# A graph layer's gather: one tile of source rows by TensorE products in two of three blocks

## The chip, the cores and the metric

The kernel runs on one core of a Trainium2 chip. The metric is the device time of one execution in microseconds (us). Three runs of the kernel before give 3887.06 us as their median (3886.89 to 3891.37).

## The reference

There are 6250 nodes with 128 features and 200,000 edges sorted by their target `dst`. Layer 0 is a graph attention layer with 8 heads of 16, layer 1 a message passing layer; each has a layer norm and a ReLU ahead of it and is added to `x`.

```python
h = relu(layernorm(x))
z = (h @ W).reshape(N, 8, 16);  el, er = sums of z * attn_l, z * attn_r over each head
e = leaky_relu(el[src] + er[dst], 0.2)
a = exp(e - segment_max(e, dst)[dst])
x = x + segment_sum(z[src] * a, dst) / max(segment_sum(a, dst), 1e-9) + bias
h = relu(layernorm(x))
sv = h @ W_up                                    # scalars and vectors of each node
w  = silu(silu(edge_feats @ A1 + b1) @ A2 + b2) @ A3
x = x + (segment_sum(products of sv[src], edge_attrs and w, dst) / 10) @ W_out
```

## The kernel before

The edges are cut into 1563 tiles of 128, and 16 tiles make a block: 98 blocks, the last one with 11 tiles. Nodes lie in 50 tiles of 128 rows (the first is shifted by 32 rows). A first stage writes the table `t0` (6368 rows of 136 numbers: z and el of each node) to DRAM. Layer 0 then runs over the blocks, writes node rows `sv` to the tables `t1` and `t1z`, and layer 1 runs over the blocks with `t1`.

What both layers spend on getting `z[src]` matters here. For each edge tile POOL issues one indirect DMA (`gather`, L833), which fetches the 128 rows that the tile's source indices name. In every third block from 3 to 95 (`by_row`) the last tile is fetched in another way: SP loads 32 row addresses at a time into registers (L1074) and issues 128 DMAs of one row each (L1078), into the buffer `r`; ACT copies them into the block's `z` (`filled`). `rows_until` spreads these DMAs over SP's program: at each half iteration it emits rows until the count for three blocks ahead is reached. `r` has three buffers, `z` five (and `z_first`).

In layer 0 the order of PE, DVE, ACT and SP is the order of the program. Iteration g of the loop works at several blocks at once, each in a later stage: 

- It starts POOL's gathers for block g+3 (`take_rows`).
- SP emits rows, the stores of a finished node tile (`node_out`, L1298, of the tile from the iteration before), the load of a tile of x (`node_rows`, L1239) and more rows.
- Block g gets its logits (`logits`: DVE adds el and er, PE transposes) and the running maxima within a segment (`maxima`, two scans on DVE).
- Block g+1 (`n1`) gets er of each edge's target. `turned` transposes the one-hot tiles `s` on PE (L1151, into `p_d`) and ACT casts them to bf16 as `d` (L1153); `er_of` multiplies `d` with er, kept as three bf16 terms (L1162); `er_sum` adds the terms.
- Block g+2 (`n2`) gets its one-hot tiles s on DVE (`ends_of`, L1097), which say which of the block's 128 targets each edge has.
- Block g-1 (`b4`) gets the maxima of its neighbours, the weights a (`weights`), z times a on DVE (`weighted`, L1229) and the sums over the targets on PE (`sums`, L1234, into `p_u`).
- Block g-2 is closed (`ended`); every second block ends a node tile, which is normalised and multiplied with W_up (`node_x` to `node_s`).

All rows of x stay in SBUF (`x_all`) from layer 0 to layer 1.

Of the kernel before, what the change touches and what calls it, by code (L numbers as in the profile page):

```python
# [741 lines left out]
def tile_even_edges(  # L742
# [88 lines left out]
    def gather(to, table, tiles, width, first=0):  # L831
        for k, t in enumerate(tiles, first):
            nc.gpsimd.indirect_dma_start(  # L833
                out=to[:, k, :width], out_offset=None, in_=table,
                in_offset=bass.IndirectOffsetOnAxis(ap=src_col[:, t : t + 1], axis=0))
        return to
# [128 lines left out]
def even_edges(tc, v):  # L965
# [7 lines left out]
    with ExitStack() as ctx:  # L973
        const = ctx.enter_context(tc.tile_pool(name="fconst", bufs=1))
        z_pool = ctx.enter_context(tc.tile_pool(name="fz", bufs=5))
        s_pool = ctx.enter_context(tc.tile_pool(name="fs", bufs=16))
# [18 lines left out]
        x_all = const.tile([P, NX, P], F32, name="fx_all")  # L995
# [8 lines left out]
        a3p = const.tile([P, 2, P], F32, name="fa3p")  # L1004
        nc.sync.dma_start(a3p, v["a3p"])
# [4 lines left out]
        wout = const.tile([P, 2, P], F32, name="fwout")  # L1010
        nc.sync.dma_start(wout, v["wout"])
        dloc = const.tile([P, NB * KB], F32, name="fdloc")
        identb = l0c.tile([P, P], BF, name="fidentb")
        nc.vector.tensor_copy(identb, ident)
# [8 lines left out]
        with tc.tile_pool(name="fbuild", bufs=1) as build:  # L1023
            d_c = build.tile([P, TU], I32, name="fd_c")
            nc.sync.dma_start(d_c, dstc)
            d_i = build.tile([P, TG, P], I32, name="fd_i")
            nc.sync.dma_start(d_i, tiles_of(dstt, P))
            q_i = build.tile([P, TG, P], I32, name="fq_i")
            nc.sync.dma_start(q_i, tiles_of(dstt, P - 1))
            nxt_i = build.tile([P, TG], I32, name="fnxt")  # L1030
            nc.sync.dma_start(nxt_i, tiles_of(dstt, 2 * P)[:, :, 0])
            off = build.tile([P, TU], F32, name="foffs")
            nc.sync.dma_start(off, nums[:, :TU])
            nc.vector.tensor_sub(dloc[:, :TU], d_c, off)


            eq = build.tile([P, TG, MC], F32, name="feq")
            nc.vector.tensor_tensor(eq[:, :, :P], d_i, q_i, OP.is_equal)
            nc.vector.memset(eq[:, :, 0:1], 0.0)
            nc.vector.memset(eq[:, :, P : P + 1], 0.0)  # L1040
            nc.vector.tensor_tensor(eq[:, :, P + 1 : 2 * P + 1], d_i,
                                    nxt_i.unsqueeze(2).to_broadcast([P, TG, P]), OP.is_equal)
            nc.vector.tensor_tensor(eq[:, :, 2 * P + 1 :], d_i,
                                    q_i[:, :, 0:1].to_broadcast([P, TG, P]), OP.is_equal)
            for g in range(TG):
                nc.scalar.activation(masks[:, g, :], eq[:, g, :], AF.Copy, bias=-BIG, scale=BIG)

            zeros = build.tile([P, NL, P], F32, name="fzeros")
            nc.vector.memset(zeros, 0.0)
            nc.sync.dma_start(t1z[LATE * P - W0 :].rearrange("(j p) f -> p j f", p=P), zeros)  # L1050
# [5 lines left out]
        with tc.tile_pool(name="fat_ps", bufs=1, space=PSUM) as at_ps:  # L1056
            col = l0c.tile([P, P], F32, name="fcol")
            n = NB - 1
            nc.vector.tensor_copy(col[:, :n], v["src_col"][:, KB - 1 : n * KB : KB])
            p_c = at_ps.tile([P, P], F32, name="p_c")  # L1060
            nc.tensor.transpose(p_c[:n], col[:, :n], ident)
            for i, w in enumerate((ZW, P)):
                nc.vector.tensor_scalar(at[i][:n], p_c[:n], float(4 * w), None, op0=OP.mult)
# [53 lines left out]

        in_order = {mybir.EngineType.PE, mybir.EngineType.DVE, mybir.EngineType.Activation,
                    mybir.EngineType.SP}
        with tc.manual_schedule(engines=in_order), \  # L1120
                tc.tile_pool(name="l0", bufs=2) as l0, \
                tc.tile_pool(name="l0n", bufs=2) as l0n, \
                tc.tile_pool(name="l0_ps", bufs=1, space=PSUM) as l0_ps:
# [3 lines left out]
            p_n = l0_ps.tile([P, 512], F32, name="p_n")  # L1127
            er_p, iota_p = p_n[:, P : 2 * P].rearrange("p (t h) -> p t h", h=H), p_n[:, 3 * P :]
            nc.scalar.copy(iota_p, iota)

# [14 lines left out]

            def turned(c, q):
                if 4 * q < c["kt"]:
                    m = min(4, c["kt"] - 4 * q)
                    p_d = l0_ps.tile([P, 4, P], F32, name="p_d", bufs=2)
                    for k in range(m):  # L1150
                        nc.tensor.transpose(p_d[:, k, :], c["s"][q][:, k, :], ident)  # L1151
                    d = c["d", q] = l0.tile([P, 4, P], BF, name="d", bufs=4)
                    nc.scalar.copy(d[:, :m], p_d[:, :m])  # L1153
# [17 lines left out]
            def logits(c, bank="pe"):  # L1171
                kt = c["kt"]
                kr = kt * H
                e_s = l0.tile([P, KB, H], F32, name="e_s")
                pe = c["pe"] = p_n if bank == "p_n" else l0_ps.tile([P, 512], F32, name=bank, bufs=2)
                nc.vector.tensor_add(e_s[:, :kt], c["z"][:, :kt, F:], c["er"][:, :kt])  # L1176
                nc.vector.scalar_tensor_tensor(e_s[:, :kt], e_s[:, :kt], 0.2, e_s[:, :kt],  # L1177
                                               op0=OP.mult, op1=OP.max)
                nc.tensor.transpose(pe[:kr, :P], e_s[:, :kt].rearrange("p t h -> p (t h)"), ident)  # L1179
# [57 lines left out]

            def node_rows(i, n):
                nc.sync.dma_start(x_all[:, i : i + n, :],  # L1239
                                  xp[i * P : (i + n) * P].rearrange("(j p) f -> p j f", p=P))  # L1240

            def with_bias(i, n):
                x_i = x_all[:, i : i + n, :]
                nc.vector.tensor_add(x_i, x_i, bias_b[:, None, :].to_broadcast([P, n, F]))

            def node_x(u):
                i, n, agg = u["i"], u["n"], u["agg"]
                x_i = x_all[:, i : i + n, :]
# [14 lines left out]
            def node_h(u):  # L1263
                i, n = u["i"], u["n"]
                rs, mr = normal(l0n, u["mv"], u["rs"], n, f"n{n}")
                xn = u["xn"] = l0n.tile([P, 2, P], F32, name="xn")
                nc.scalar.activation(xn[:, 0, :], x_all[:, i, :], AF.Identity, bias=mr[:, 0, :],
                                     scale=rs[:, 0, :])
                if n == 2:
                    nc.vector.tensor_scalar(xn[:, 1, :], x_all[:, i + 1, :], u["mv"][:, 1, 0:1],  # L1270
                                            rs[:, 1, :], op0=OP.subtract, op1=OP.mult)

            def node_t(u):
                n = u["n"]
                u["p_n"] = p_n.rearrange("p (j f) -> p j f", f=P)
                for j in range(n):
                    nc.tensor.transpose(u["p_n"][:, j, :], u["xn"][:, j, :], ident)
                h_t = u["h_t"] = l0n.tile([P, 2, P], F32, name="h_t")
                nc.scalar.activation(h_t[:, :n], u["p_n"][:, :n], AF.Relu)
# [11 lines left out]
            def node_out(u):  # L1291
                i, n, sv = u["i"], u["n"], u["sv"]
                first = i * P - W0
                for table in (t1, t1z) if i < LATE else (t1,):
                    if i == 0:
                        nc.sync.dma_start(table[: P - W0, :], sv[W0:, 0, :])
                    else:
                        nc.sync.dma_start(  # L1298
                            table[first : first + n * P].rearrange("(j p) f -> p j f", p=P), sv)

# [12 lines left out]
            def take_rows(g):  # L1313
                if 0 < g < NG:
                    c = cs[g]
                    t = c["b"] * KB + c["o"]
                    c["z"] = gathered(t0, range(t, t + c["kt"] - (c["b"] in by_row)), ZW)
# [28 lines left out]
            for g in range(1, 3):  # L1346
                take_rows(g)
            masks_of(cs[0])
# [12 lines left out]
            for i in range(2):  # L1361
                node_rows(i, 1)
            for g in range(NG - 3):
# [3 lines left out]
                for n in late:  # L1367
                    node_out(n)
                if g % 2 == 0 and g // 2 + 2 < NX - 2:
# [6 lines left out]
                logits(c)  # L1376
                ends_of(n2, 0)
# [3 lines left out]
                maxima(c)  # L1381
                ends_of(n2, 1)
# [5 lines left out]
                er_of(n1, 0)  # L1388
                if b4:
                    weights(b4)  # L1390
                for n in nodes:
# [3 lines left out]
                if b4:  # L1395
                    bank_of(b4)
                    weighted(b4, 0)
                turned(n1, 3)
                er_of(n1, 2)
                if b4:  # L1400
                    weighted(b4, 8)
                for n in nodes:
# [4 lines left out]
                if b4:  # L1407
                    sums(b4, 0)
                for n in nodes:
# [7 lines left out]
                if b4:  # L1417
                    sums(b4, 8)
                if g == NG - 4:
# [68 lines left out]
        with tc.manual_schedule(engines=in_order), \  # L1488
                tc.tile_pool(name="l1", bufs=3) as l1, \
                tc.tile_pool(name="l1n", bufs=2) as l1n, \  # L1490
                tc.tile_pool(name="l1_ps", bufs=2, space=PSUM) as l1_ps:

# [79 lines left out]

            def node1(i, agg):
                x_i = x_all[:, i, :]
# [10 lines left out]
            def node_out1(i):  # L1585
                x_i = x_all[:, i, :]
                if i == 0:
                    nc.sync.dma_start(out[: P - W0, :], x_all[W0:, 0, :])
# [54 lines left out]
            rows, rows_until.n, late = rows_by_row(1, t1, P), 0, []  # L1643
# [13 lines left out]
            for i, u in enumerate(us):  # L1657
                b, k0, m = u["b"], u["k0"], u["m"]
                if k0 == 0:
                    take_rows(b + 2)  # L1660
                    filled(1, b, blk[b]["z"], P)
                    edge_rows(b + 2)
                if k0 == 4:
# [43 lines left out]
            x_i = x_all[:, NX - 2 :, :]  # L1707
# [140 lines left out]
```

## Time and profile before

| | us |
|---|---|
| median of three runs | 3887.06 |
| the profiled execution | 3888.67 |
| its span, first to last instruction | 3886.9 |
| POOL busy / PE busy / DVE busy / ACT busy | 2913.0 / 2848.8 / 2224.5 / 1396.8 |
| layer 0's first logits / last block's gathers begin | 91.7 / 1945 |
| layer 1's first gather from `t1` | 1989.4 |
| mean granted clock of TensorE | 0.803 |

In the profile, PE is TensorE's matmuls, PEld its weight loads, DVE VectorE, ACT ScalarE, POOL GpSimd and SP SyncE; "SPq" marks a DMA that SP issues. Busy time leaves out the issuing of DMAs by SP. A line of a group reads: line of the kernel, engine, operation, output<-input, count, then busy us and mean ns of one, then the idle time of the engine just before and what ended it.

### The profile page before, as it was taken

Reading aid. Unit: us, or ns where it says so; the run is one execution under the profiler, and the core shown is the slowest. Engines: PE = TensorE matmul, PEld = TensorE weight load, DVE = VectorE, ACT = ScalarE, POOL = GpSimd, SP = SyncE. Lnnn points to the kernel's source line nnn. Section 1 sums busy time; section 2 is a strip of 40 time slices with the busy share of each in tenths; the row PEclk is TensorE's granted clock in tenths of the full one; section 3 lists DMA queues with packets and bytes.
Section 4 is the critical chain, followed back from the end, with each engine's and each line's share of the span. In section 5 each row is a group of like instructions: output and inputs, shape, how many; then the busy total and the mean of one; then the engine's idle time right before and its main releaser. Section 6 shows DMA issues by size and latency. Waiting matters only on the chain. (4 is left out here: it accounts for less than half of the span.)

```text
span 3886.9 us, 62701 instructions
## 1 busy us (share of the span) xinstructions
PE 2848.8 (73%) x14785; PEld 2401.2 (62%) x14785; DVE 2224.5 (57%) x5408; ACT 1396.8 (36%) x3612; POOL 2913.0 (75%) x3096
## 2 busy tenths in 40 slices
PE   3766666666666766666678888888877777778777
PEld 3656656656556656666666666666666556656665
DVE  5544444444444444444457777677766666666666
ACT  3323232323322323232324444444444444444443
POOL 6777777777777777777777777777777777777776
PEclk6666666666666566666689999999999999999999
DMA  6222222222222222222222222222222222222221
GB/s 181 59 64 64 62 64 64 64 62 64 62 64 62 64 61 64 62 64 62 61 61 61 61 62 62 62 62 62 62 62 62 62 62 61 63 60 63 61 61 50
DMA packets 195262, 252.65 MB, mean 65 GB/s; under 512 B 78656, under 2 KB 145088, under 8 KB 194880
## 3 DMA queue, kind: packets, MB, share of 16 engines
q0 software_dynamic: 98048, 207.27, 22.6%
q1 hardware_dynamic: 96544, 41.19, 4.1%
q8 instruction: 120, 1.97, 0.2%
q14 instruction: 262, 2.15, 0.2%
q10 hardware_dynamic: 288, 0.07, 0.0%
HBM read 234.73 MB, written 13.25 MB: 64 GB/s over the span
## 5 line engine op out<-in xcount | busy, mean ns | idle before, releaser
L833 POOL DMA_INDIRECT g<-ft,fsrc x3024 | 2856.7, 945 | 922.4 <-issue 858.3
L1570 PE MATMUL p_u<-mj,s 128*128 128x256 f32 x3126 | 789.9, 397 | 217.9 <-DVE mj L1562 216.5
L1570 PEld LDWEIGHTS p_u<-mj,s 128*128 128x128 f32 x3126 | 588.9, 196 | 385.7 <-DVE mj L1562 310.9
L1234 PE MATMUL p_u<-g,s 128*128 128x136 f32 x3062 | 597.8, 376 | 0.4 <-DVE g L1229 0.4
L1234 PEld LDWEIGHTS p_u<-g,s 128*128 128x128 f32 x3062 | 572.1, 279 | 0.5 <-DVE g L1229 0.4
L1537 ACT ACTIVATE p_w<-p_w,yb 128x64 f32<-128x64 f32 x1563 | 450.3, 288 | 121.5 <-PE p_w L1533 80.4
L1553 DVE TENSOR_TENSOR vy<-g,p_i 128x384 f32<-128x384 f32 x387 | 212.9, 550 | 366.6 <-DMA g<-ft,fsrc 258.0
L1533 PE MATMUL p_w<-fa3p,h 128*128 128x256 f32 x1564 | 412.0, 387 | 0.0
L1151 PE MATMUL p_d<-fident,s 128*128 128x128 f32 x1563 | 384.7, 411 | 0.0
L1533 PEld LDWEIGHTS p_w<-fa3p,h 128*128 128x128 f32 x1564 | 289.4, 195 | 118.1 <-issue 52.5
L1176 DVE TENSOR_TENSOR e_s<-g,p_n 128x128 f32<-128x128 f32 x96 | 27.5, 286 | 578.6 <-DMA g<-ft,fsrc 566.2
L1518 ACT ACTIVATE h<-p_h,fb 128x512 f32<-128x512 f32 x196 | 134.6, 687 | 573.2 <-PE p_h L1516 571.8
L1151 PEld LDWEIGHTS p_d<-fident,s 128*128 128x128 f32 x1563 | 312.4, 225 | 37.6 <-issue 26.3
L1144 ACT COPY mk<-p_m 128x385 f32<-128x385 f32 (+1 forms) x99 | 47.6, 481 | 781.3 <-PE p_m L1141 781.2
L1229 DVE TENSOR_TENSOR g<-g,pe 128x1024 f32<-128x1024 f32 x193 | 225.5, 1209 | 129.2 <-ACT g L1220 126.4
L1153 ACT CAST d<-p_d 128x512 bf16<-128x512 f32 x391 | 228.8, 586 | 192.0 <-PE p_d L1151 141.6
L1179 PE MATMUL pe<-fident,e_s 128*128 128x128 f32 x98 | 39.1, 399 | 326.2 <-DVE e_s L1177 326.2
L1097 DVE TENSOR_TENSOR s<-p_n,fdloc 128x512 f32<-128x512 f32 x391 | 266.1, 682 | 6.7 <-ACT sv L1289 3.4
L1097 DVE TENSOR_TENSOR s<-p_i,fdloc 128x512 f32<-128x512 f32 x391 | 266.1, 681 | 3.8 <-ACT p_i L1512 3.8
L1516 PE MATMUL p_h<-ft,fa1p 128*128 128x128 f32 x1568 | 217.2, 283 | 63.3 <-DMA ft<-in_e_f_dram 63.1
L1516 PEld LDWEIGHTS p_h<-ft,fa1p 128*128 128x128 f32 x1568 | 210.6, 198 | 83.9 <-issue 65.3
L1523 ACT ACTIVATE h<-p_h,fb 128x512 f32<-128x512 f32 x196 | 134.7, 687 | 307.1 <-PE p_h L1520 307.1
(202 smaller groups left out, 3344.3 us busy)
## 6 DMA issues: line engine op xcount, KB each, us to landing
r<-ft SPq DMA_DIRECT2D x3968, 0.5 KB
r<-ft SPq DMA_DIRECT2D x3968, 0.5 KB
g<-ft,fsrc POOLq DMA_INDIRECT x3024
ft<-in_e_f_dram SPq DMA_DIRECT2D x98, 64.0 KB
yb<-in_e_y_dram SPq DMA_DIRECT2D x98, 32.0 KB
fx_all<-in_e_xp_dram SPq DMA_DIRECT2D x48, 64.0 KB
out_dram<-fx_all SPq DMA_DIRECT2D x47, 64.0 KB
ft<-sv SPq DMA_DIRECT2D x46, 64.0 KB
```

Of the source, the lines that this page charges most:

```text
L833: nc.gpsimd.indirect_dma_start(out=to[:, k, :width], out_offset=None, in_=table, in_offset=bass.IndirectOffsetOnAxis(ap=src_col[:, t : t + ...
L1097: nc.vector.tensor_tensor(s[:, :m], iota[:, None, :].to_broadcast([P, m, P]), dloc[:, t : t + m].unsqueeze(2).to_broadcast([P, m, P]), OP. ...
L1151: nc.tensor.transpose(p_d[:, k, :], c["s"][q][:, k, :], ident)
L1153: nc.scalar.copy(d[:, :m], p_d[:, :m])
L1229: nc.vector.tensor_mul(zh, zh, p_a[:, k0 : k0 + m].unsqueeze(3).to_broadcast([P, m, H, D]))
L1234: nc.tensor.matmul(c["p_u"][:, :ZW], c["s"][k // 4][:, k % 4, :], c["z"][:, k, :], start=c["o"] + k == 0, stop=c["o"] + k == KT[c["b"]] - 1)
L1516: nc.tensor.matmul(p_h[:, q, :], a1p[:, q0 + q, :], c["ft"], start=True, stop=True)
L1523: nc.scalar.activation(h2, p_h, AF.Silu, bias=b2)
L1533: nc.tensor.matmul(w[:, k : k + n].rearrange("p k a u -> p (k a u)"), c["h2"][q // 4][:, q % 4, :], a3p[:, :n].rearrange("p k f -> p (k f) ...
L1537: nc.scalar.activation(w[:, k, ::2, :], w[:, k, ::2, :], AF.Copy, scale=c["yb"][:, k0 + k, 0:1])
L1553: nc.vector.tensor_mul(vy, v_n, y_p)
L1570: nc.tensor.matmul(blk[b]["p_u"][:, :MW], u["s"][:, k, :], u["mj"][:, k, :], start=k0 + k == 0, stop=k0 + k == KT[b] - 1)
```

## The change

In layer 0, blocks 28 to 92 that are not in `by_row` are `dense`: 44 blocks. Their tile 14 is no longer gathered. Its rows are computed by products of one-hot tiles with the table itself, which lies in SBUF as `t0s`, each number split into three bf16 terms.

- `node_tiles(g + 1)` loads two tiles of 128 table rows per iteration from DRAM, one iteration ahead; `split(g)` makes the three terms of them at the iteration's end (two copies on ACT, two subtractions on DVE). This goes on for the first 25 pairs.
- For a dense block, `spread` (PE) writes the tile's source indices across all partitions, folded into a third of the table; `ends_to` (DVE, twice) makes 17 one-hot tiles; `rows_of` (PE) runs 17 x 3 matmuls, each with up to three table tiles (408 columns) beside each other, into the PSUM bank `p_x`; `taken` (DVE) picks of the three thirds the right one and writes the tile's `z`. A block's first 27 matmuls run two iterations before its logits, the other 24 and `taken` one before.
- To free two PSUM banks, `turned` changes in all blocks: a table `ends` of local target numbers is written to DRAM once at the start (`d_b`); `ends_row(b)` loads the block's 16 x 128 numbers to every partition by a DMA on SP (4 KB to each of 128 partitions), two buffers; DVE compares them with each partition's own number and writes `d` in bf16. The transposes on PE and the casts on ACT are gone.
- To free SBUF, `x_all` is gone: tiles of x come in buffers, are stored to DRAM (`x1`) behind the node's stores and are loaded again in layer 1 (`node_rows1`). `a3p` and `wout` are loaded at the start of layer 1.
- `er_p` and the iota move to the bank `p_i`; `p_n` is allocated for each node.

```diff
+        dense = {b for b in range(NX // 2 + 2, NB - 4) if b not in by_row}
+            def ends_row(b):
+                if b < NB:
+                    to = ends_row.tiles[b] = l0.tile([P, KB, P], BF, name="er_d", bufs=2)
+                    g, j = divmod(b, P // KB)
+                    nc.sync.dma_start(to, ends[g : g + 1, j * KB : (j + 1) * KB, :].to_broadcast([P, KB, P]))
             def turned(c, q):
                 if 4 * q < c["kt"]:
                     m = min(4, c["kt"] - 4 * q)
-                    p_d = l0_ps.tile([P, 4, P], F32, name="p_d", bufs=2)
-                    for k in range(m):
-                        nc.tensor.transpose(p_d[:, k, :], c["s"][q][:, k, :], ident)
-                    d = c["d", q] = l0.tile([P, 4, P], BF, name="d", bufs=4)
-                    nc.scalar.copy(d[:, :m], p_d[:, :m])
+                    d = c["d", q] = l0.tile([P, 4, P], BF, name="d")
+                    k0 = c["o"] + 4 * q
+                    nc.vector.tensor_tensor(d[:, :m], ends_row.tiles[c["b"]][:, k0 : k0 + m],
+                                            node_p.unsqueeze(2).to_broadcast([P, m, P]), OP.is_equal)
+            def spread(c):
+                b = c["b"]
+                nc.tensor.matmul(at_p, key[:, b : b + 1].to_broadcast([P, P]), ident,
+                                 start=True, stop=True)
+            def ends_to(c, h):
+                n = half if h == 0 else NR - half
+                oh = c["oh", h] = ohs[:, h * half : (h + 1) * half, :]
+                nc.vector.tensor_tensor(
+                    oh[:, :n], at_p.unsqueeze(1).to_broadcast([P, n, P]),
+                    place[:, h * half : h * half + n].unsqueeze(2).to_broadcast([P, n, P]), OP.is_equal)
+            def rows_of(c, k0, n):
+                if k0 == 0:
+                    p_x = l0_ps.tile([P, 512], F32, name="p_x")
+                    c["p_x"] = p_x[:, : 3 * ZW].rearrange("p (r f) -> p r f", f=ZW)
+                for k in range(k0, min(k0 + n, NR)):
+                    i = order[k]
+                    m = len(range(i, NX, NR))
+                    for s in range(3):
+                        nc.tensor.matmul(c["p_x"][:, :m, :], c["oh", k // half][:, k % half, :],
+                                         t0s[:, s, i::NR, :], start=k == 0 and s == 0,
+                                         stop=k == NR - 1 and s == 2)
+            def taken(c):
+                b, z = c["b"], c["z"][:, KD, :]
+                nc.vector.tensor_scalar(z, c["p_x"][:, 0, :], part[:, b, 0:1], None, op0=OP.mult)
+                for r in (1, 2):
+                    nc.vector.scalar_tensor_tensor(z, c["p_x"][:, r, :], part[:, b, r : r + 1], z,
+                                                   op0=OP.mult, op1=OP.add)
@@ take_rows
-                    c["z"] = gathered(t0, range(t, t + c["kt"] - (c["b"] in by_row)), ZW)
+                    c["z"] = gathered(t0, [k for k in range(t, t + c["kt"])
+                                           if not (c["b"] in by_row and k % KB == KB - 1)
+                                           and not (c["b"] in dense and k % KB == KD)], ZW)
@@ node_out
+                nc.sync.dma_start(x1[i : i + n].rearrange("j p f -> p j f"), x_of.pop(i))
@@ the loop of layer 0
                 for n in late:
                     node_out(n)
+                node_tiles(g + 1)
                 if g % 2 == 0 and g // 2 + 2 < NX - 2:
                     node_rows(g // 2 + 2, 1)
                 rows_until(rows, g + 1)
...
                 logits(c)
+                ends_row(g + 2)
+                to, was = n2["b"] in dense, n1["b"] in dense
+                if to:
+                    spread(n2)
                 ends_of(n2, 0)
                 if n1 is not none:
                     masks_of(n1)
                 turned(n1, 0)
                 maxima(c)
+                if to:
+                    ends_to(n2, 0)
+                if was:
+                    rows_of(n1, half, 4)
...
                 er_of(n1, 0)
+                if was:
+                    rows_of(n1, half + 4, NR)
                 if b4:
                     weights(b4)
+                if was:
+                    taken(n1)
...
                 if b4:
                     weighted(b4, 0)
+                if to:
+                    ends_to(n2, 1)
...
+                if to:
+                    rows_of(n2, 0, 3)
...
+                if to:
+                    rows_of(n2, 3, 3)
...
                 if b4:
                     sums(b4, 8)
+                if to:
+                    rows_of(n2, 6, half - 6)
+                split(g)
```

## The prediction, made before the result was known

> **What bounds the kernel now.** I read the page, the waits, then the timelines of POOL and of SP's queue.
>
> ```profile
> PE 2848.8 (73%) x14785; PEld 2401.2 (62%) x14785; DVE 2224.5 (57%) x5408; ACT 1396.8 (36%) x3612; POOL 2913.0 (75%) x3096
> PEclk6666666666666566666689999999999999999999
> L833 POOL DMA_INDIRECT g<-ft,fsrc x3024 | 2856.7, 945 | 922.4 <-issue 858.3
> L1234 PE MATMUL p_u<-g,s 128*128 128x136 f32 x3062 | 597.8, 376 | 0.4 <-DVE g L1229 0.4
> ```
>
> POOL shows 75%, yet it is the bound: between its gathers it waits for nothing but "issue". From 1200 to 1800 us it issued 481, one per 600/481 = 1.247 us, and so everywhere. A group of three layer-0 blocks has 47 gathers, 58.6 us (19.53 a block). The logits of a block wait for its last gather (6.1 us a block on DVE), so compute has slack. A removed gather is worth 1.247 us while POOL keeps the pace.
>
> SP's queue counts as nothing in part 1, so I read its timeline (start, duration, instruction).
>
> ```profile
> 70.93 59.43 SPq L1078 DMA_DIRECT2D r<-ft  x152
> 130.42 0.38 SPq L1239 DMA_DIRECT2D fx_all<-in_e_xp_dram  x1
> ...
> 234.90 0.38 SPq L1298 DMA_DIRECT2D ft<-sv  x1
> 235.34 0.42 SPq L1298 DMA_DIRECT2D ft1z<-sv  x1
> 235.81 0.42 SPq L1239 DMA_DIRECT2D fx_all<-in_e_xp_dram  x1
> 236.33 34.34 SPq L1078 DMA_DIRECT2D r<-ft  x84
> 270.77 0.38 SPq L1298 DMA_DIRECT2D ft<-sv  x1
> ```
>
> SP is full: single rows at 0.323 us, 2.2 us for each load of 32 addresses. It sends the sv at 234.90 that ACT had ready long before:
>
> ```profile
> 181.42 0.28 ACT L1289 ACTIVATE sv<-p_n 128x128 f32<-128x128 f32 x1 [2.28 <-PE p_n L1284]
> ```
>
> It is 53 us behind because it emits 152 rows (60 us) before anything else of the loop. It catches up late; the first long gap ahead of a node store is 4.1 us, after the row at 840.93:
>
> ```profile
> 833.79 7.37 SPq L1078 DMA_DIRECT2D r<-ft  x23
> 845.29 0.38 SPq L1298 DMA_DIRECT2D ft<-sv  x1
> ```
>
> So SP's own pace is (841.2 - 234.9)/34 blocks = 17.83 us a block, 91% of POOL's. In layer 0 its lag costs nothing now: rows are fetched three blocks ahead, and stores are not urgent. Where compute does need an SP load soon, it already waits (layer 1):
>
> ```profile
> PE p_h L1516 <- DMA ft<-in_e_f_dram: 63.1, 27, 5.1
> ```
>
> **The skill.** "DMA: Bandwidth & Descriptors", section "Anatomy of one DMA", fits a DMA's time as 2.0 us + bytes/436e3 (a software-queue fit). 64 KB gives 2.15 us; in layer 1 PE starts mostly 2.05 to 2.2 us after the issue of a 64 KB ft, so the trace agrees. "TensorE: Matmul & The Clock Gate", section "Back-to-back issue gap", gives N/1.2 ns cold and N/2.4 + 2.5 ns warm per matmul. The trace shows two such paces: 16 matmuls of p_u took 3.68 us, the next 16 took 2.02 us.
>
> **The change, part by part.**
>
> Gathers: blocks 28 to 92 that are no multiple of three are 44, one gather less each: 44 x 1.247 = 54.9 us less POOL time.
>
> TensorE rows: 17 one-hot tiles x 3 terms = 51 bf16 matmuls of 408 columns per dense block, split 27 and 24 over two iterations. By the skill's prices 408 columns are 0.17 us warm, 0.34 cold: 8.8 to 17.3 us a dense block. The 16 transposes of s (L1151, 0.244 us each in a run of 8) go from all blocks: -3.9. An iteration with both halves has about 9 us of other PE work warm, 13.5 cold: 18 to 31 us in all; the other two of three 13 to 22. PE will be busier and, I take it, mostly warm: mean about 15 us.
>
> DVE: now 9 us a block. turned adds 4 comparisons of 128x512 (like L1097, 0.68): +2.7. A dense block adds ends_to (1152 and 1024 columns, like L1229's 1.21 for 1024): +2.5; taken, three of 136 columns at 0.29: +0.9. About 16 us where all meet, a mean of 14.5, plus 2 to 3 us of waits: below SP's pace. ACT loses 4 x 0.586. The splits (two tiles for 25 blocks, about 0.45 us an operation) lie at the iteration's end, in the former gather wait.
>
> SP: this decides. Per block it gains ends_row (about 0.50 us to issue, priced by the 0.42 us stores here plus the gap and a semaphore wait); every second block the store of x1 (0.53, so 0.26); and in the first 25 blocks node_tiles (0.50). In the built program each DMA of SP waits for the one eight before it, which shares its semaphore. ends_row writes 512 KB (4 KB to each partition): 2.0 + 1.2 = 3.2 us by the fit, 3.4 with the gathers' 24% of the DMA engines added to the second term. The eighth DMA after it, mostly a row, would start 0.5 + 7 x 0.323 = 2.8 us later, so SP stalls about 0.6 us. In one of three blocks an address load (2.2 us) comes right behind ends_row and hides it: 0.4 us a block. Sum: 17.83 + 0.50 + 0.26 + 0.50 + 0.40 = 19.5 us while tiles are split, then 19.0. POOL's new pace there is 45/3 x 1.247 = 18.7. SP becomes the slower one.
>
> And now its lag matters: turned(n1) stands early in DVE's order, ahead of the logits' maxima, and waits for ends_row, which SP issues behind all rows of the iteration. Behind DVE stand scan, weights and sums, then PE, and POOL's buffers. At the start: SP's rows begin near 83 us (68.6 now; d_b and its 1664-run store come first, and both ends_row wait for that store). ends_row(2) is issued at 83 + 61.8 (as now) + 9.6 (22 rows, one load, two issues) = 154.4. Its block's turned runs in iteration 1, which starts at 99.9 now. Then ends_row(91), the last behind rows, is issued at 154.4 + 23 x 19.5 + 66 x 19.0 = 1857, landing near 1860; with unrounded terms 1858.5. The same iteration (90) starts at 1828.6 now: compute is 30 us late although POOL has less to do.
>
> After that SP is free. POOL's gathers for block 93 begin as iteration 90 does (five buffers, so block k waits for iteration k-4 to end): 15 + 16 + 16 + 16 + 11 tiles and 24 early ones for layer 1 are 98 x 1.247 = 122 us, so the first gather from the second table falls at 1981 instead of 1989.4. Layer 1 is bound by POOL as before: SP's load of x1 there (0.47 us every second block) keeps its pace of 18.4 us below 19.5. The a3p and wout loads only move. **Sum: about -8 us.**
>
> The profiled execution took 3888.67 us, its span 3886.9; the median of the runs is 3887.06. The sum on the profiled one gives 3881, against the median 3879, which I take.
>
> **The rivals.**
>
> 1. SP keeps up or isn't waited for; POOL sets the pace. For it: SP is issue-bound and the ring stall is only estimated. Against it: the 53 us lag is there before anything is added. -55 us: 3832. Without the stall, but SP-paced, it is -8 - 89 x 0.4 = about -43, at most.
>
> 2. Slower: ends_row lands late. All 128 partitions read the same 4 KB of DRAM beside the gathers, and the row loads queue behind it. Each further us of landing costs 89 x 2/3 = 59 us. A landing of 4.2 us gives a stall of 1.4 and +40: 3927. It is slower by over 0.2% from a landing of about 3.7 us on. For it: in the start phase, fa1p, as large, was awaited 5.5 us after its issue, beside other loads. Against it: those loads.
>
> 3. The compute chain becomes the bound: PE stays cold, or taken waits for rows_of and so delays weighted and sums. For it: PEclk 0.6 in layer 0. Against it: with fuller PE the clock should rise, as in layer 1. Half a us over SP's pace in 66 blocks: +33, with -8 about 3912.
>
> **How the numbers follow.** 0.2% is 7.8 us, about what a measurement of this kernel can tell from no change. Case SP-paced with a stall of 0.3 to 0.9 us: 0.50; its own range is 3858 to 3897 and it splits 0.28 faster, 0.15 same, 0.07 slower. Rival 1: 0.12, faster. Rival 2: 0.27, slower. Rival 3: 0.11, of which 0.02 same, 0.09 slower. Together faster 0.40, same 0.17, slower 0.43. The likeliest single time is 3879; the range 3838 to 3926 leaves out most of rival 1 at the bottom and the far end of 2 and 3.
>
> **What would show it.** Right: in layer 0 DVE's comparison in turned waits for the er_d load; node stores on SP no longer wait for ACT between 845 and 1825 us; iterations start 19.5, later 19.0 us apart, the second near 157 us; POOL shows waits for buffers; the gap after ends_row's eighth DMA is about 0.6 us. Wrong: POOL still waits for "issue" alone (rival 1), the gap is over 1 us (rival 2), or SP waits for sv again while DVE or PE has no gap (rival 3).

## The result and the profile after

The change made the kernel slower: 3929.23 us (median of 4, 3927.07 to 3932.46) against 3887.32 before (3886.89 to 3891.37); ratio 1.0105 [1.0089, 1.0121]. The forecast was 3879 with a range up to 3926. The profiled execution after took 3928.91 us, its span 3927.1. In after, the gather is L834, the rows of SP L1082, `one_hot` L1101, `spread` L1197, `ends_row` L1252, `turned` L1261, the node stores L1410, layer 1's products with `ft` L1661.

The page of after, the lines that answer to those of before:

```profile
PE 2769.8 (71%) x15554; PEld 2180.9 (56%) x15554; DVE 2622.5 (67%) x6094; ACT 1200.4 (31%) x3272; POOL 2873.1 (73%) x3052
PEclk6566667888888888788879999999999999999998
L834 POOL DMA_INDIRECT g<-ft,fsrc x2980 | 2816.8, 945 | 998.6 <-issue 908.5
L1343 PE MATMUL p_u<-g,s 128*128 128x136 f32 x3062 | 509.8, 335 | 0.4 <-DVE g L1338 0.4
```

The 44 gathers are gone: POOL is busy 39.9 us less. But its idle time before gathers grew by 76 us, so it no longer sets the pace. TensorE executes 769 matmuls more, and its granted clock in layer 0 rises from .6 to .8 where the dense blocks begin.

SP's timeline (start, duration, instruction) where layer 0 begins; `er_d` is the tile that ends_row fills, and `r<-ft` are the rows:

```profile
72.91 0.37 SPq L1037 DMA_DIRECT2D fends_d<-fd_b  x1
81.53 0.81 SPq L1252 DMA_DIRECT2D er_d<-fends_d  x2
...
87.53 58.61 SPq L1082 DMA_DIRECT2D r<-ft  x152
...
147.22 8.72 SPq L1082 DMA_DIRECT2D r<-ft  x20
156.03 0.36 SPq L1252 DMA_DIRECT2D er_d<-fends_d  x1
```

The third ends_row goes out at 156.03 us, behind 172 rows. VectorE's timeline shows who waits for it; the bracket is the idle time ahead of the instruction and what ended it:

```profile
159.97 0.69 DVE L1261 TENSOR_TENSOR d<-er_d,p_i 128x512 bf16<-128x512 bf16 x1 [56.33 <-DMA er_d<-fends_d]
```

The waits of after (us in total, times, longest):

```profile
POOL g L834 <- issue: 910.6, 2793, 4.7
DVE d L1261 <- DMA er_d<-fends_d: 282.9, 65, 56.3
DVE s L1101 <- PE p_i L1197: 141.9, 44, 4.5
PE p_h L1661 <- DMA ft<-in_e_f_dram: 90.7, 33, 5.4
POOL g L834 <- PE pe L1304: 28.3, 1, 28.3
```

65 of 98 blocks wait for ends_row. POOL stands still for 28.3 us near the start: its five buffers are full and compute is stuck behind ends_row. Layer 1's wait for `ft` (63.1 before) is larger, but layer 1 is not longer: from the first gather of `t1` to the last gather it takes 1881.6 us in both traces. The whole loss lies ahead of that first gather.

The waits of SP's queue in after between 1200 and 1800 us, where the time of a block is steady:

```profile
SPq L1082 <- DMA er_d<-fends_d: 26.7, 20, 2.2
```

20 times in some 31 blocks a row waited for an ends_row sent eight DMAs earlier, whose semaphore it uses (below, this wait is the stall): 1.34 us each, 0.87 us a block.

Where the logits of a block start (first `e_s` on VectorE) tells the lag and the pace of every kernel below. Each ratio is to the runs of before on the same chip: 3895.9 us on that of no_dense, er_top, ahead1 and er_act, 3887 to 3889 us on the others, and 6292 us on the one on which the four kernels with `_b` ran a first time, from which nothing is read.

| kernel | time us | ratio to before | block 2 | block 90 | blocks 58 to 90, us each |
|---|---|---|---|---|---|
| before | 3887.3 | | 111.9 | 1828.6 | 19.55 |
| after | 3929.2 | 1.0105 [1.0089, 1.0121] | 171.1 | 1896.3 | 19.48 |
| no_dense | 3932.8 | 1.0099 [1.0083, 1.0116] | 171.6 | 1889.8 | 19.40 |
| er_top | 3917.5 | 1.0058 [1.0041, 1.0074] | 156.8 | 1879.8 | 19.45 |
| ahead1 | 3892.7 | 0.9993 [0.9984, 1.0001] | 138.5 | 1857.4 | 19.44 |
| er_act | 4141.7 | 1.0632 [1.0614, 1.065] | 160.6 | 2095.1 | 23.37 |
| er_load | 3862.0 | 0.9932 [0.9916, 0.9949] | 157.3 | 1826.7 | 18.75 |
| er_load_ahead1 | 3835.4 | 0.9863 [0.9846, 0.9879] | 121.6 | 1791.8 | 18.75 |
| er_half | 3888.5 | 1.0001 [0.9992, 1.001] | 171.1 | 1854.4 | 19.03 |
| er_double | 4264.6 | 1.0968 [1.095, 1.0987] | 183.8 | 2226.1 | 23.14 |
| fix_no_dense_b | 3891.0 | 1.0007 [0.9998, 1.0015] | 121.8 | 1831.3 | 19.56 |
| fix_all_dense_b | 3943.7 | 1.0141 [1.0124, 1.0158] | 122.0 | 1907.8 | 20.59 |
| before_ahead1_b | 3889.1 | 1.0002 [0.9993, 1.0011] | 111.0 | 1827.1 | 19.53 |
| er_pool_b | 3939.2 | 1.013 [1.011, 1.015] | 184.9 | 1884.4 | 19.38 |

### The profile page after: what moved, and what is told of

The parts are those of the page before. It is cut to its first block, busy times and chain, and to the rows that moved or that the text cites. A ratio compares the mean times of both kernels' runs of the same rounds, so it can differ in the third digit from the quotient of the medians.

```text
span 3927.1 us, 64767 instructions
## 1 busy us (share of the span) xinstructions
PE 2769.8 (71%) x15554; PEld 2180.9 (56%) x15554; DVE 2622.5 (67%) x6094; ACT 1200.4 (31%) x3272; POOL 2873.1 (73%) x3052
## 5 line engine op out<-in xcount | busy, mean ns | idle before, releaser
L834 POOL DMA_INDIRECT g<-ft,fsrc x2980 | 2816.8, 945 | 998.6 <-issue 908.5
L1101 DVE TENSOR_TENSOR s<-p_i,fdloc 128x512 f32<-128x512 f32 x782 | 533.5, 683 | 149.0 <-PE p_i L1197 141.9
L1343 PE MATMUL p_u<-g,s 128*128 128x136 f32 x3062 | 509.8, 335 | 0.4 <-DVE g L1338 0.4
L1343 PEld LDWEIGHTS p_u<-g,s 128*128 128x128 f32 x3062 | 484.8, 240 | 2.1 <-DVE g L1338 0.4
L1221 PE MATMUL p_x<-t0s,fz_first 128*128 128x408 bf16 (+1 forms) x2244 | 460.0, 358 | 0.0
L1261 DVE TENSOR_TENSOR d<-er_d,p_i 128x512 bf16<-128x512 bf16 x391 | 264.2, 676 | 284.4 <-DMA er_d<-fends_d 282.9
L1221 PEld LDWEIGHTS <-fz_first 128*128 128x128 bf16 x2244 | 225.6, 103 | 153.4 <-issue 24.6
L1661 PE MATMUL p_h<-ft,fa1p 128*128 128x128 f32 x1568 | 223.0, 288 | 90.8 <-DMA ft<-in_e_f_dram 90.7
L1661 PEld LDWEIGHTS p_h<-ft,fa1p 128*128 128x128 f32 x1568 | 214.3, 202 | 113.5 <-issue 99.2
L1271 PEld LDWEIGHTS <-d 128*128 128x128 bf16 x1563 | 95.4, 115 | 264.8 <-DVE d L1261 260.7
L1312 PE MATMUL pe<-mx,fshift 128*128 128x1 f32 (+1 forms) x194 | 43.6, 294 | 272.8 <-ACT mx L1298 272.5
L1702 DVE TENSOR_REDUCE vd<-vy 128x128 f32<-128x384 f32 x391 | 228.9, 585 | 0.0
L1700 DVE TENSOR_TENSOR p_w<-g,p_w 128x128 f32<-128x128 f32 x387 | 112.5, 291 | 161.2 <-ACT p_w L1682 141.4
```

The lines of the kernel that those rows point to most:

```text
L834: nc.gpsimd.indirect_dma_start(out=to[:, k, :width], out_offset=None, in_=table, in_offset=bass.IndirectOffsetOnAxis(ap=src_col[:, t : t + ...
L1101: nc.vector.tensor_tensor(s[:, :m], iota[:, None, :].to_broadcast([P, m, P]), dloc[:, t : t + m].unsqueeze(2).to_broadcast([P, m, P]), OP. ...
L1221: nc.tensor.matmul(c["p_x"][:, :m, :], c["oh", k // half][:, k % half, :], t0s[:, s, i::NR, :], start=k == 0 and s == 0, stop=k == NR - 1 ...
L1261: nc.vector.tensor_tensor(d[:, :m], ends_row.tiles[c["b"]][:, k0 : k0 + m], node_p.unsqueeze(2).to_broadcast([P, m, P]), OP.is_equal)
L1343: nc.tensor.matmul(c["p_u"][:, :ZW], c["s"][k // 4][:, k % 4, :], c["z"][:, k, :], start=c["o"] + k == 0, stop=c["o"] + k == KT[c["b"]] - 1)
L1661: nc.tensor.matmul(p_h[:, q, :], a1p[:, q0 + q, :], c["ft"], start=True, stop=True)
```

## The experiments

Each starts from after, unless it says otherwise. The letters S, C, P, D and R are the explanations that the expectations set against each other; S and C are told in the first one.

**no_dense: are the removed gathers worth anything?**

```diff
-        dense = {b for b in range(NX // 2 + 2, NB - 4) if b not in by_row}
+        dense = set()
```

> No block is dense: all gathers back on POOL (47 per three blocks, 19.53 us a block), no one-hot rows on TensorE, the rest as after. Theory S (SP's pace, 19.5 us a block, plus its 56 us of rows at the start sets layer 0; the 44 gathers were removed from beside the path): 3925 to 3940, because SP's program is unchanged. Rival C (the comparisons, products and waits of the dense blocks lengthen the compute chain, which sets the pace): the 40 us go away, 3885 to 3900. Rival P (POOL still sets the time and the gathers have become slower): +55, 3985.

3932.8 us, as theory S has it: after with its gathers back is as slow as after. Its waits from 1200 to 1800 us:

```profile
DVE d L1261 <- DMA er_d<-fends_d: 201.1, 31, 9.3
POOL g L834 <- issue: 139.7, 458, 0.3
```

Without dense work VectorE simply waits longer for ends_row, in every block. But the run alone doesn't rule out C for after. With 47 gathers in three blocks POOL has no wait above 0.3 us here: its own pace, 19.53 us a block, is nearly SP's, so blocks could not have followed each other much faster in any case. What rules C out are er_half and er_load below, which keep all dense work and take 19.03 and 18.75 us a block.

**er_top: the load ahead of the rows.**

```diff
                 take_rows(g + 3)
+                ends_row(g + 2)
                 filled(0, g, cs[g]["z"], ZW)
...
                 logits(c)
-                ends_row(g + 2)
```

> ends_row(g + 2) is issued by SP at the top of iteration g, ahead of its rows, not behind them; SP's work is otherwise the same. Theory S: the pace stays 19.5 us a block with the stall, and only the start gains: ends_row(2) comes before the 149 rows and ends_row(3) right behind them (about 148 us, in place of 176), so everything is one block of rows earlier: about -25 us, 3895 to 3910. If the stall needs rows right behind ends_row, it is still there (rows follow now too). Rival C: no change, 3925 to 3933.

Block 2 is 14.3 us earlier, block 90 16.5, the span 16.6; the pace is the same. The direction is S's, the size less than the 25 expected. ends_row(3) goes out at 162.03 us (174.95 in after) and not near 148: the expectation left out the 20 rows in the second half of iteration 0, and the first rows start 5.6 us later than in after, behind an ends_row that waits 4.3 us for its buffer. The stalls are all there (26.5 us in 20, from 1200 to 1800), since rows follow ends_row here too.

**ahead1: fewer rows at the start.**

```diff
-                rows_until(rows, g + 0.5)
+                rows_until(rows, g - 1.5)
...
-                rows_until(rows, g + 1)
+                rows_until(rows, g - 1)
```

> Rows in layer 0 are sent one block ahead of their block instead of three: 85 rows and their address loads (some 33 us of SP) move from the start to the end of layer 0; the pace of SP in between is unchanged. Theory S: the lag of SP at the start falls by 33 us and the whole of layer 0 with it: 3890 to 3902. Rival C (compute chain sets the pace): no change, 3925 to 3933. Rival R: rows now come late for their own block and the gain is lost in waits of the row copy on ACT: 3910 to 3930.

Block 2 starts 32.6 us earlier and the span is 36.8 us shorter, at an unchanged pace: what is lost at the start is carried to the end. SP's lag is on the path.

**er_act: another queue.**

```diff
-                    nc.sync.dma_start(to, ends[g : g + 1, ...
+                    nc.scalar.dma_start(to, ends[g : g + 1, ...
```

> ends_row is issued from ACT's queue, where it stands ahead of the mask copy, not behind SP's rows. Theory S: SP is freed of 0.50 us and of the stall of 0.87 us a block and nobody waits for its lag any more; POOL's 18.7 us a block is next: 3832 to 3850. Rival C (compute chain, with the wait of the one-hot of block n2 for the spread on PE, 4.5 us in each of 44 iterations): 3880 to 3930. Rival D (the 512 KB of loads slow the gathers): no better than after, 3920 or more.

4141.7 us, far above what S and C allow; only D ("3920 or more") is open that far. Waits of the whole execution, SP's queue first and then ACT:

```profile
SPq L1082 <- DMA er_d<-fends_d: 381.5, 80, 11.9
```

```profile
ACT g L1096 <- DMA r<-ft: 240.4, 34, 16.6
ACT sv L1401 <- DMA ft1z<-sv: 125.3, 13, 13.7
```

SP sends no ends_row here, and yet its rows wait for it, up to 11.9 us. In the built program the DMAs of SP and ACT take the same eight semaphores in turn, in the order of the program; the trace's records show eight for SP and ACT together and eight others for POOL. A row that comes eight places behind an ends_row waits until ACT has come to that ends_row; ACT in its turn waits for rows and for node stores of SP. The Trainium skill ("DMA: Bandwidth & Descriptors", section "Issuing engines are not separate DMA queues") says that a second issuing engine saves only the time to issue; here it cost some 205 us against after (by the two ratios), with these waits. D is not the reason: er_load_ahead1 below loads the same bytes, and its POOL issues 481 gathers from 1200 to 1800 us, as many as before. The test of the tie is the next run.

**er_pool_b: a queue with semaphores of its own** (`nc.gpsimd.dma_start` in the same place).

> As er_act, but ends_row is issued on POOL's queue, whose DMAs have eight semaphores of their own and share none with SP's rows. If er_act was slow because SP's rows and ACT's ends_row take the same eight semaphores in turn and so hold each other up, this one isn't: POOL pays some 1.0 to 1.5 us for each ends_row in 89 blocks, 3920 to 3970, and SP shows no wait for er_d. If any queue beside SP is bad for it (its landing, or its place behind compute): 4050 or more.

3939.2 us. The largest wait of SP's queue in it, and then POOL's timeline around an ends_row:

```profile
SPq L1410 <- ACT sv L1401: 172.5, 23, 38.3
```

```profile
1205.11 0.94 POOL L834 DMA_INDIRECT g<-ft,fsrc  x1 [0.30 <-issue]
1206.05 0.59 POOL L1252 DMA_DIRECT2D er_d<-fends_d  x1
1206.94 0.98 POOL L834 DMA_INDIRECT g<-ft,fsrc  x1 [0.30 <-issue]
```

SP waits for ACT's results and never for er_d: it has time again. POOL pays 0.58 us (two gathers start 1.83 us apart instead of 1.25), less than expected. Its first logits come at 164.5 us, because POOL emits the first two ends_row behind the gathers of two blocks. A second queue that shares no semaphore with SP holds up none of its DMAs; with the waits shown above, the shared semaphores are what made er_act slow.

**er_load: something long behind the load.** The first load of 32 addresses in an iteration follows ends_row directly.

```diff
                     if e % 32 == 0:
+                        if ends_row_due:
+                            ends_row_due.pop()()
...
                 take_rows(g + 3)
+                ends_row_due.append(lambda b=g + 2: ends_row(b))
...
                 logits(c)
-                ends_row(g + 2)
+                if ends_row_due:
+                    ends_row_due.pop()()
```

> SP issues ends_row(g + 2) right ahead of the first load of 32 addresses that falls in iteration g (there is one in every iteration), so that the 2.2 us of that load lie between ends_row and the rows behind it. Theory S with the stall as its second half: the wait of the eighth DMA behind ends_row (0.87 us a block) is hidden, SP's pace falls to about 19.2 us, later 18.6, and the start gains 14 us as in er_top: iteration 90 near 1807 in place of 1896, total 3835 to 3855. Rival C (the chain of comparisons, products and the wait for the spread needs about 19.5 us in dense blocks anyway): only the 14 us of the start, 3910 to 3918.

3862.0 us, faster than before, 7 us above the expectation. Here L1084 is a row and L1254 ends_row. Waits of SP's queue from 1200 to 1800 us, then of POOL in the whole execution:

```profile
SPq L1084 <- DMA er_d<-fends_d: 0.8, 1, 0.8
```

```profile
POOL g L834 <- issue: 841.8, 2756, 1.4
POOL g L834 <- DVE pe L1296: 25.7, 10, 23.0
```

The stall is gone and the pace is POOL's 18.75. er_top has nearly the same block 2 and differs in what follows ends_row (and in when it is sent within an iteration): the 51.6 us between the two spans (49 by the ratios) are what the stall cost, up to where POOL takes over. The 23.0 us are POOL's standstill with full buffers at the start. POOL sets the pace afterwards, so they are never made good; the expectation had SP catch up.

**er_load_ahead1: both causes taken away** (the two edits together).

> er_load with the rows sent one block ahead in place of three. Theory S: SP no longer lags, POOL's 18.7 us a block is the bound again, the 54.9 us of removed gathers come out whole: 3830 to 3842. Rival C: as ahead1, 3885 to 3895.

3835.4 us, 1.4% less than before. The largest wait of POOL, whole execution:

```profile
POOL g L834 <- issue: 835.4, 2739, 0.3
```

No gather has waited for a buffer. This is the version that beats both.

**fix_no_dense_b, fix_all_dense_b: er_load_ahead1 with other dense blocks.**

```diff
+        dense = set()                                   # fix_no_dense_b
+        dense = set(range(NX // 2 + 2, NB - 4))         # fix_all_dense_b
```

> er_load_ahead1 with no dense block (all 44 gathers back on POOL, no one-hot rows on TensorE). Theory S: with SP off the path POOL's 19.53 us a block is the bound, so the gathers are worth their full 54.9 us here: 3883 to 3895, against 3835. Rival C: what er_load_ahead1 gained comes from elsewhere than the gathers, and dense blocks stay worth little, as between no_dense and after: 3835 to 3850.

> er_load_ahead1 with every block from the 28th to the 93rd dense, those with rows from SP included (22 gathers less, 27 us of POOL). POOL's pace there would be 18.3 us a block. Theory S: SP's 17.83 + 0.50 + 0.26 = 18.6 is then the bound: 3815 to 3828. Rival C: with products and comparisons of a dense block in every iteration the chain of DVE and TensorE takes longer than 18.75 us: 3836 to 3900.

Without dense blocks 3891.0 us: the 44 gathers are worth 55.6 us here, the 54.9 of the prediction's first step. With every block from 27 to 93 dense 3943.7, more than even C expected: rival C is true of this kernel. Its waits from 1200 to 1800 us:

```profile
POOL g L834 <- issue: 186.5, 402, 5.1
DVE s L1103 <- PE p_i L1199: 129.6, 29, 6.2
```

In every block VectorE now waits 4.5 us for the spread, which TensorE reaches only after the earlier block's products; POOL has waits of up to 5.1 us ahead of gathers. The chain takes 20.6 us a block, and with 23 gathers less the kernel is 108 us slower than er_load_ahead1.

**before_ahead1_b: the kernel before, with the edit of ahead1.**

> The kernel before with rows sent one block ahead in place of three. Theory S: SP's lag was hidden by POOL there, no change: 3884 to 3891. If the late rows or stores cost anything in the kernel before, it gains as ahead1 did: 3850 to 3865.

No change (1.0002). The same rows cost nothing while nobody waits for what SP sends behind them.

**er_half and er_double: the size of the landing.** er_half loads 8 of the 16 tiles, and the comparisons of all 16 read these, so that the number of instructions stays and the result is not the layer's; er_double sends each ends_row twice into the same tile.

```diff
+    nc.sync.dma_start(to, ends[g : g + 1, j * KB : j * KB + KB // 2, :]...)      # er_half
+    for _ in range(2): nc.sync.dma_start(to, ends[g : g + 1, ...])                # er_double
```

> As after, but ends_row loads the first 8 of the 16 edge tiles of its block alone (256 KB), and every comparison of turned reads from these; the logits of the other tiles are not computed from their own ends. Theory S with a landing that grows with the bytes: about 0.6 us less landing, half or more of the 1.34 us stalls gone, 0.5 to 0.87 us a block: 3852 to 3885. If the landing is latency and not bytes: 3925 to 3933. Rival C: the same.

> As after, but each ends_row load is issued twice into the same tile. Theory S: per block 0.5 us more to issue and a second landing that the eighth DMA behind it waits for, together 1.3 to 1.8 us for 89 blocks: 4045 to 4090. Rival C: SP has room, 3930 to 3945.

Waits of SP's queue, er_half from 1200 to 1800 us, then er_double, whole execution (L1253 is ends_row there):

```profile
SPq L1082 <- DMA er_d<-fends_d: 12.7, 20, 1.0
```

```profile
SPq L1253 <- DMA er_d<-fends_d: 328.8, 97, 4.9
SPq L1082 <- DMA er_d<-fends_d: 63.1, 60, 1.8
```

er_half: the same 20 stalls, 0.64 us each in place of 1.34, and a span 41.6 us shorter, just outside its expectation. By the stalls, half the bytes land 0.70 us earlier, which gives an estimate of 374 GB/s (262,144 bytes in 0.70 us). er_double came out far above its 4045 to 4090. It was meant to add one landing beside the other, but the second load writes the tile that the first one writes and so waits for all of it: 3.39 us, plus 0.5 to issue, in each block. The sum of 3.9 us, less what the stalls of the rows became smaller (63.1 us in all, 79.4 in after), gives about the 335 us by which it is slower, 3.7 us in each of some 90 blocks. The run measures the landing instead: about 0.4 + 3.4 = 3.8 us.

## Why the prediction was wrong

**Right: what sets layer 0.** SP's own pace and its lag at the start, with `turned` waiting for an ends_row behind the rows. ends_row(2) was forecast for 154.4 us and issued at 156.03. SP's terms 17.83 + 0.50 + 0.26 stood as a sum: 19.48 us a block less the stall of 0.87 leaves 18.61. er_top, ahead1 and er_load show the causal side.

**Right: the gathers' price.** 54.9 us forecast, 55.6 measured, once SP is off the path.

**Right: compute has room.** VectorE was put at a mean of 14.5 us a block and TensorE at 15; from 1000 to 1850 us they are busy 592.73 and 603.60 us of 850, that is 13.6 and 13.8 us of 19.48. TensorE was mostly warm: from start to start the products of 408 columns take 0.173 us (median), the 0.17 of the prediction. Rival 3 was not what happened.

**Wrong: the term for the ring stall.** The step "SP stalls about 0.6 us", from a landing of 3.4 us, was mis-sized: measured 1.34 us, a landing of 0.5 + 7 x 0.323 + 1.34 = 4.1 us. At two of three blocks that is 0.87 us, not 0.40, and the sum 17.83 + 0.50 + 0.26 + 0.87 = 19.46 us is the pace seen (19.5). Over 89 blocks 0.47 us more make 42 us; the other terms together came out some 4 us smaller, and iteration 90 began at 1896.3, not at 1858.5. (A small part is a slip in the sum: 1.2 us with 24% added is 1.5, so the text's own working gives 3.5 us and not 3.4.) This is rival 2, given 27 in 100, whose landing of 4.2 us and +40 us are nearly the values found. By er_half the miss lies in the part that doesn't depend on the bytes: at the estimated 374 GB/s 512 KB take 1.4 us, and 4.1 - 1.4 leaves 2.7 us where the fit of the skill ("DMA: Bandwidth & Descriptors", "Anatomy of one DMA", a fit to the software queue) has 2.0. At 59 us for each us of landing, these 0.7 us are the sign of the result. The text's own mark for rival 2, a gap of over 1 us after ends_row's eighth DMA, is what the trace shows.

Rival 2 also gave reasons for a late landing, and the traces allow a look at them. They record when a DMA's last semaphore update came. The medians from issue to that update in layer 0 after 150 us, by what SP does right behind the load (of the loads whose records are complete, their number in brackets):

| load | KB | the fit (estimate) | a row behind | a load of 32 addresses behind |
|---|---|---|---|---|
| tile of x, L1351, after | 64 | 2.15 | 2.22 (21) | 2.25 (13) |
| two table tiles, L1179, after | 136 | 2.32 | 2.29 (7) | |
| ends_row, L1253, er_half | 256 | 2.60 | 3.35 (59) | 3.33 (26) |
| ends_row, L1252, after | 512 | 3.20 | 3.97 (60) | 3.95 (25) |

Rows behind a load don't delay its landing, and the tiles of x and of the table, sent by the same queue beside the same gathers, keep to the fit (2.64 us for 8 loads of table tiles with a tile of x right behind). ends_row is about 0.75 us above it at both sizes. So the miss goes with this load, and not with the queue, the rows or the gathers in general: checking the fit with a 64 KB load of another kind couldn't show it.

**Wrong, smaller: the tail.** From iteration 90 to the first gather of `t1` 122 us were forecast; it took 2028.9 - 1896.3 = 132.6. POOL waited there once 4.6 us ahead of the first early gather into `fz_first` (by the trace until a store of x) and once 4.05 us right ahead of the first gather of `t1`; neither was in the sum. The first in the waits of POOL in after:

```profile
POOL fz_first L834 <- DMA fx<-x: 4.6, 1, 4.6
```

Together: -8 + 38 + 10 = +40 us, which is the difference of the profiled executions (3928.91 - 3888.67).

What isn't settled is which property of ends_row costs the 0.75 us. It differs from the other loads in two ways at least: all 128 partitions read the same few KB of DRAM, and each gets 2 or 4 KB. No run takes these apart; a load of as many bytes from 512 KB of DRAM in its place would.

## What to carry to other kernels

When an engine gets a load that compute needs soon, look at two things ahead of its price: what the issuing queue has still to send before it, and what the eighth DMA behind it finds. A lag that cost nothing while nobody waited becomes the path in full, and is carried to the end when the next slowest engine has no speed to spare; a few tenths of a us in a queue that is issue-bound count once for each block. Put something long that the queue has to do anyway (here a load of addresses into registers) right behind the big transfer, and don't send the transfer from a second engine whose DMAs take semaphores in turn with the first one's. Check the price of a load with one of the same kind, not with a smaller one of another kind.

## What the hardware showed

- A 512 KB load that spreads 4 KB of DRAM over 128 partitions landed about 4.0 us after its issue from SP (median in after), with a row or an address load behind it; half of it landed after 3.35 us (er_half). Loads of 64 and 136 KB from the same queue landed after 2.2 and 2.3 us.
- Issued from ACT, the 512 KB load held up SP's rows by up to 11.9 us, through the semaphores that both queues use in turn; issued from POOL, it held up none, cost POOL 0.58 us and landed after 4.5 us.
- With the 51 products of 408 bf16 columns in each dense block, TensorE is busy 72% of the time from 1200 to 1800 us and its granted clock there is 0.85; without them (no_dense) it is busy 44% and the clock is 0.67. In the kernel before these are 67% and 0.65.
